# A graph-attention layer beside a dot-product layer: a list scheduler in the source orders the engines, and layer 1's value products go in halves among its scores

## The chip, the cores and the metric

The kernel runs on one core of one Trainium2 chip. The metric is the device time of one execution in microseconds. The core has a tensor engine (PE, with its weight loads shown as PEld), a vector engine (DVE), a scalar engine (ACT), GpSimd (POOL) and a sync engine (SP) that issues most DMAs. Each engine takes its instructions in the order in which the program wrote them.

## The reference

Eight entries (B = 8) of 2048 nodes with 256 channels pass through two layers, all in float32. `adj` is one 2048 x 2048 matrix of 0 and 1.

```python
# layer 0: eight heads of 32 channels, additive scores
x_proj = einsum('bnd,hdf->bhnf', x, W)
e = leaky_relu(e_src[..., :, None] + e_dst[..., None, :], 0.2)
e = e + softplus(beta_tilde) * log(adj + 1e-6)
attn = softmax(where(adj > 0, e, -big), axis=-1)
h = einsum('bhij,bhjf->bhif', attn, x_proj)        # heads side by side
x = layernorm(x + h @ W_out.T)
# layer 1: one head of 256 channels, dot-product scores
h1, h2, h3 = x @ W1, x @ W2, x @ W3
e = where(adj > 0, leaky_relu(h1 @ h2.T, 0.2), -1e12)
x = layernorm(x + relu(softmax(e, axis=-1) @ h3))
```

## The kernel before

**Layer 0** is cut into units. A unit is one entry, a pair of heads (`hp`, four of them) and one half of the 2048 rows (`rh`), so an entry has 8 units. A unit has 16 steps (`jt`), one for each block of 128 source nodes. A step has a tile `s` of 128 x 2 x 1024: for 11 of the 16 steps ACT first scales a mask tile `mt` that SP has loaded (L491, once per head), DVE then forms the attention weights from `c`, `re` and the scaled tile (L505, once per head), and POOL adds them into `sums` (L511, once per head). The other five steps are "direct": they skip ACT and POOL. PE takes each step with `products` (L537): four matmuls of 32 columns for the values (`val`) and, for a direct step, four more for the denominators (`den`). These are the **strips**. At a unit's end four more strips with `ones` close the sums (`close`). Seven `s` tiles are in use at most, four `mt` tiles, and `c` lies in two PSUM tiles that ACT fills once per unit (L501).

**Layer 1** goes row tile by row tile, 16 in an entry. A row tile has four score tiles (`e`, L715, full-width matmuls of 512 columns), each taken out of PSUM by ACT with the leaky ReLU (L717). DVE masks the row and finds its maximum (L724), ACT takes the exponential (L727). PE then transposes the result in four groups (`pt`, L743), ACT copies each out (`pts`, L745), and 16 products with `h3` add up in one PSUM tile (`acc`, L765). The row ends with a ReLU, a sum and a layernorm on ACT and DVE (L766 to L790).

Between the entries lies the **seam**: the output projection `y` of layer 0 (L411), its sum and layernorm (L415 to L439, and a store `x_d` issued from ACT's queue at L441), the transposes `tr` (L458) and `h3p` (L464), and the first query tiles (`h1p`, L704).

Layer 0 of entry 0 runs alone. From then on layer 1 of entry b-1 and layer 0 of entry b share the engines, in an order that is written out by hand: `Dot.step` writes for each quarter of a row tile a transpose of this row tile, a score tile of the next, and then `stream.feed()`, which takes one layer-0 step and makes another.

```python
self.scores(it + 1, lambda c: (turned(c), stream.scale_head() if c else None),
            lambda c: (stream.feed(), stream.scale_next(2) if c == NB - 1 else None))
...
for n in (7, 7, 7, 7, 6, 8, 7, 7, 7, 7, 8, 6, 7, 7):
    dot.step(stream, n)
```

The 16 products of `acc` follow in one piece after the fourth score tile. Full-width results rotate through two PSUM banks; the other six hold `val`, `den` and the two `c` tiles. Layer 1 of entry 7 has no layer 0 beside it, and there the two banks become six.

Of the kernel before, what the change touches and what calls it, by code (L numbers as in the profile page):

```python
# [18 lines left out]
P = 128  # L19
# [8 lines left out]
def kernel(  # L28
# [41 lines left out]
    LEAD = 3  # L70
    AHEAD = 1
# [8 lines left out]
    ps = ctx.enter_context(tc.tile_pool(name="ps", bufs=2, space=PSUM))  # L80
    pacc = ctx.enter_context(tc.tile_pool(name="pacc", bufs=1, space=PSUM))

    banks = ["mm"]

    def mm_tile(name):
        tag = banks[0]
        banks.append(banks.pop(0))
        if tag == "mm":
            return ps.tile([P, BK], F32, tag="mm", name=name)
        return pacc.tile([P, BK], F32, tag=tag, name=name)  # L90
# [139 lines left out]

    def mask(it, make):

        pen = wide_tile("pen", "pen", 1, BF16)
        if not make:
            nc.sync.dma_start(pen, pen_d[ts(it, P), :])
            return pen, lambda: None
        edges = [chunk.tile([P, HALF], I32, tag="ht", name="adj_r", bufs=4) for _ in range(2)]
        for s, a in enumerate(edges):
            nc.sync.dma_start(a, adj[ts(it, P), ts(s, HALF)])

        def put():
            nc.scalar.activation(pen[:, ts(0, HALF)], edges[0], AF.Relu, bias=no_edge, scale=-NO_EDGE)
            nc.vector.tensor_scalar(pen[:, ts(1, HALF)], edges[1], 0.0, NO_EDGE, ALU.is_le, ALU.mult)
            nc.sync.dma_start(pen_d[ts(it, P), :], pen)
        return pen, put
# [17 lines left out]
    class Gat:  # L263
# [132 lines left out]
        def load_rows(self, g):  # L396

            if g < NB:
                xg = chunk.tile([P, IG, D], F32, tag="ht", name="xg", bufs=4)
                nc.sync.dma_start(xg, x[self.b].rearrange("(t p) d -> p t d", p=P)[:, ts(g, IG), :])  # L400
                self.xs = getattr(self, "xs", []) + [xg]

        def rows(self, g):


            self.load_rows(g + 2)
            self.st = st = small.tile([P, IG // 2, nc.vector.BN_STATS_DIM], F32, name="st4", bufs=2)
            ys = [mm_tile("y").rearrange("p (t c) -> p t c", t=2) for _ in range(IG // 2)]
            for k in range(IG):
                for kc in range(KC):  # L410
                    nc.tensor.matmul(ys[k // 2][:, k % 2, :], self.ht[kc][:, ts(g * IG + k, P)], wot[:, kc, :],  # L411
                                     start=(kc == 0), stop=(kc == KC - 1))
            for k, y in enumerate(ys):
                z = self.x1(2 * g + k)
                nc.vector.tensor_add(z, y, self.xs[g][:, ts(k, 2), :])  # L415
            self.rows_factor()
            for k in range(len(ys)):
                nc.vector.bn_stats(st[:, k, :], self.x1(2 * g + k).rearrange("p t c -> p c t"))

        def rows_scale(self):  # L420

            self.mv = mv = self.st.rearrange("p a (t c) -> p (a t) c", t=2)
            self.f = f = small.tile([P, 2, IG], F32, name="f4", bufs=2)
            nc.scalar.activation(f[:, 0, :], mv[:, :, 2], AF.Ln, bias=eps_ln, scale=1.0 / D)
            nc.scalar.activation(f[:, 0, :], f[:, 0, :], AF.Exp, scale=-0.5)

        def rows_factor(self):

            if self.mv is not None:
                nc.vector.scalar_tensor_tensor(self.f[:, 1, :], self.mv[:, :, 1], -1.0, self.f[:, 0, :], ALU.mult, ALU.mult)  # L430
                self.mv = None

        def rows_end(self, g):

            self.rows_factor()
            for k in range(IG):
                z, f = self.x1(2 * g + k // 2), self.f
                row = z[:, k % 2, :]
                nc.scalar.activation(row, row, AF.Identity, bias=f[:, 1, k:k + 1], scale=f[:, 0, k:k + 1])  # L439
                if k % 2:  # L440
                    nc.scalar.dma_start(x1_d[self.b].rearrange("(t p) d -> p t d", p=P)[:, ts(2 * g + k // 2, 2), :], z)  # L441

# [3 lines left out]

        def turn(self):


            self.x1t = x1t = whole.tile([P, KC, N], F32, tag="x1t", name="x1t")  # L450
            self.h3 = h3 = whole.tile([P, NT, D], F32, tag="h3", name="h3")
            lag = 2 if self.b + 1 < B else 4
            for j in range(NT // 2 + lag):
                if j < NT // 2:
                    t = mm_tile("tr1")
                    for kc in range(KC):
                        for i in range(2):
                            nc.tensor.transpose(t[:, ts(kc * 2 + i, P)], self.x1(j)[:, i, ts(kc, P)], ident)  # L458
                    nc.scalar.copy(x1t[:, :, ts(j, 2 * P)], t.rearrange("p (k i) -> p k i", k=KC))
                if j >= lag:  # L460
                    t = mm_tile("h3p")
                    for i in range(2):
                        for kc in range(KC):
                            nc.tensor.matmul(t[:, ts(i, D)], x1t[:, kc, ts(2 * (j - lag) + i, P)], w3s[:, kc, :],  # L464
                                             start=(kc == 0), stop=(kc == KC - 1))
                    nc.scalar.copy(h3[:, ts(j - lag, 2), :], t.rearrange("p (i c) -> p i c", i=2))
                if j > 0:
                    yield

# [132 lines left out]
    class Stream:  # L602


        def __init__(self):
            self.units = [Unit(gats[b], hp, rh) for b in range(1, B) for hp in range(NP) for rh in range(2)]
            self.count = len(self.units) * NT
            self.loaded = self.scaled = self.made = self.eaten = 0
            self.held, self.heads = False, 0
            self.mts = {}  # L610

        def at(self, n):
            return self.units[n // NT], n % NT

        def load(self, upto):

            while self.loaded < min(upto, self.count):
                n = self.loaded
                self.mts[n] = load_mt(n // 2 % NT, n % 2)
                self.loaded += 1  # L620

        def scale_head(self, ahead=AHEAD):

            if self.heads == 0 and self.scaled < min(self.made + 1 + ahead, self.count, self.eaten + SLOTS):
                assert self.scaled - self.eaten < SLOTS
                unit, jt = self.at(self.scaled)
                unit.begin(jt, self.mts.pop(self.scaled))
                unit.scale(jt, 0)
                self.heads = 1

        def scale_next(self, ahead=AHEAD):

            self.scale_head(ahead)
            if self.heads:
                unit, jt = self.at(self.scaled)
                for a in range(1, HP):
                    unit.scale(jt, a)
                self.heads = 0
                self.scaled += 1

        def make_next(self):

            unit, jt = self.at(self.made)
            unit.make(jt)
            if jt == 4:
                stage_after(unit)
            self.made += 1
            self.load(self.made + 4)

        def ahead(self, count=1):  # L650

            for _ in range(count):
                self.scale_next()
                if self.made == self.scaled:
                    continue
                if self.made % NT == 0 and self.made and not self.held:
                    self.held = True
                    continue
                self.make_next()
                if self.held:  # L660
                    self.held = False
                    self.scale_next()
                    self.make_next()

        def eat(self, count=1):

            for _ in range(min(count, self.count - self.eaten)):
                unit, jt = self.at(self.eaten)
                assert self.eaten < self.made
                unit.eat(jt)  # L670
                evict()
                if jt == 0 and self.eaten > 0:
                    self.at(self.eaten - 1)[0].close()
                self.eaten += 1
                if self.eaten == self.count:
                    unit.close()
                if self.eaten % 2 == 0:
                    tick()
                    k = unit.rh * J2 + jt // 2
                    unit.gat.next_values(unit.hp, k)  # L680
# [9 lines left out]
    class Dot:  # L690
# [17 lines left out]
        def scores(self, it, between=lambda c: None, after=lambda c: None):  # L708

            (pen, put), p = mask(it, self.b == 0), self.p  # L710
            for c in range(NB):
# [6 lines left out]
                if c == 2:  # L718
                    put()
# [241 lines left out]
```

## Time and profile before

| | us |
|---|---|
| median of 3 runs | 4308.99 (4303.66 to 4311.37) |
| the profiled execution, its own time | 4305.87 |
| its span, first to last instruction | 4304.1 |
| PE busy | 4111.9 (96%) |
| DVE busy | 3257.0 (76%) |
| ACT busy | 2932.1 (68%) |
| POOL busy | 2910.7 (68%) |

Busy time of PE is the union of its matmuls, whose ends are modelled: a matmul that starts a little late because the array was being changed over does not show as idle. The starts of matmuls in the timeline are the better measure. A group line gives busy time, the mean duration of one instruction in ns, and the idle time of the engine before it with what ended that.

### The profile page before, as it was taken

The page shows a single profiled execution, that of the slowest core. Times are in us where ns is not written, and L with a number is a line of the kernel's source. Part 1 is how long each engine was busy: PE and PEld are TensorE (multiplying, and loading weights), DVE is VectorE, ACT ScalarE, POOL GpSimd, SP SyncE. Part 2 cuts the span into 40 slices and gives each one's busy share as a digit, 9 for nine tenths or more (in the row PEclk, how much of TensorE's full clock was granted, in tenths as well). Part 3 has the DMA queues.
Part 4 walks back from the last instruction along what each step waited for, and adds up shares of the span by engine and source line. Part 5 has one row for each costly group of instructions (what it writes and reads, how often), then busy time and mean ns, then how long its engine had stood idle before and what let it go on. Part 6 is the DMA issues. An engine that isn't in the chain of part 4 may idle for free.

```text
span 4304.1 us, 60568 instructions
## 1 busy us (share of the span) xinstructions
PE 4111.9 (96%) x22704; PEld 2073.5 (48%) x22704; DVE 3257.0 (76%) x3391; ACT 2932.1 (68%) x4148; POOL 2910.7 (68%) x1190
## 2 busy tenths in 40 slices
PE   7999889999999999999899999999899999999999
PEld 4444334444444444445444454444444444444766
DVE  7888878888787878788777878788787877787222
ACT  6522377777777767777777767778677776776555
POOL 0000468988788877889788878888788888888000
PEclk9999999999999999999999999999999999999999
DMA  7888756776565556556556665656566665664211
GB/s 257 280 287 291 235 188 231 231 233 225 186 204 189 190 192 200 189 188 225 177 186 201 198 203 183 200 183 207 194 203 193 197 205 180 192 200 145 74 47 47
DMA packets 346439, 843.65 MB, mean 196 GB/s; under 512 B 49696, under 2 KB 166432, under 8 KB 346144
## 3 DMA queue, kind: packets, MB, share of 16 engines
q1 hardware_dynamic: 328736, 822.99, 58.9%
q10 hardware_dynamic: 17408, 16.78, 1.2%
q8 instruction: 178, 2.92, 0.3%
q14 instruction: 117, 0.96, 0.1%
HBM read 763.76 MB, written 75.37 MB: 195 GB/s over the span
## 4 chain that ended last, share of the span: by engine, by line
PE 71%; ACT 10%; DVE 7%; DMA 6%; issue 4%; SPq 1%; ACTq 1%; POOL 0%; DVEq 0%; POOLq 0%
PE acc L765 18%; PE e L715 18%; PE val L537 16%; PE den L537 6%; PE pt L743 5%; ACT s L491 4%; DVE s L505 4%; DMA mt<-mt_d 3%; PE h1p L704 3%; PE y L411 2%; DVE p L724 2%; PE proj L296 1%; ACT c L501 1%; ACT ht L439 1%; PE h3p L464 1%
## 5 line engine op out<-in xcount | busy, mean ns | idle before, releaser
L511 POOL TENSOR_TENSOR sums<-sums,s 128x1024 f32<-128x1024 f32 x1008 | 2520.4, 2537 | 165.3 <-DVE s L505 164.3
L505 DVE SCALAR_TENSOR_TENSOR s<-c,re,s 128x1024 f32<-128x1024 f32 x1232 | 1502.5, 1273 | 316.9 <-ACT c L501 251.4
L491 ACT ACTIVATE s<-mt,re 128x1024 f32<-128x1024 f32 x1232 | 1358.7, 1143 | 92.8 <-DMA mt<-mt_d 76.2
L537 PE MATMUL val<-s,v 128*32 128x512 f32 x8192 | 1116.0, 607 | 81.6 <-DVE s L505 74.9
L715 PE MATMUL e<-x1t,h 128*128 128x512 f32 x2048 | 973.2, 598 | 20.7 <-ACT p L717 11.4
L765 PE MATMUL acc<-h,pts 128*128 128x256 f32 x4096 | 916.4, 382 | 4.4 <-ACT pts L745 4.3
L765 PEld LDWEIGHTS acc<-h,pts 128*128 128x128 f32 x4096 | 769.0, 190 | 200.6 <-ACT p L717 38.6
L505 DVE SCALAR_TENSOR_TENSOR s<-c,re,mt 128x1024 f32<-128x1024 f32 x560 | 688.3, 1271 | 0.2
L724 DVE CUSTOM_DVE_ANT_0 p<-p,pen 128x2048 f32<-128x2048 f32 x128 | 415.8, 3248 | 357.0 <-ACT p L717 356.9
L511 POOL TENSOR_TENSOR sums<-s 128x1024 f32<-128x1024 f32 x112 | 292.6, 2634 | 426.4 <-DVE s L505 419.2
L537 PEld LDWEIGHTS val<-s,v 128*32 128x32 f32 x8192 | 203.0, 109 | 746.4 <-issue 430.2
L715 PEld LDWEIGHTS e<-x1t,h 128*128 128x128 f32 x2048 | 348.4, 190 | 300.7 <-issue 248.0
L717 ACT ACTIVATE p<-e 128x512 f32<-128x512 f32 x512 | 305.4, 597 | 268.4 <-PE e L715 260.3
L537 PE MATMUL den<-s,re 128*32 128x512 f32 x3264 | 440.7, 593 | 0.0
L743 PEld LDWEIGHTS pt<-ident,p 128*128 128x128 f32 x2048 | 220.2, 141 | 424.1 <-ACT p L717 148.4
L745 ACT COPY pts<-pt 128x512 f32<-128x512 f32 x512 | 295.1, 580 | 145.0 <-PE pt L743 144.2
L727 ACT ACTIVATE p<-p,neg 128x2048 f32<-128x2048 f32 x128 | 256.1, 2001 | 199.3 <-DVE neg L725 148.4
L743 PE MATMUL pt<-ident,p 128*128 128x128 f32 x2048 | 328.6, 284 | 36.8 <-ACT pts L745 28.0
L505 DVE SCALAR_TENSOR_TENSOR s<-c_in,re,mt 128x1024 f32<-128x1024 f32 x256 | 310.1, 1277 | 48.5 <-DMA mt<-mt_d 35.9
L307 POOL PARTITION_ALL_REDUCE top<-top x8 | 6.6, 819 | 431.2 <-DVE top L306 414.6
L537 PEld LDWEIGHTS den<-s,re 128*32 128x32 f32 x3264 | 109.6, 110 | 244.5 <-issue 242.5
L298 ACT COPY v<-proj 128x512 f32<-128x512 f32 x64 | 37.2, 585 | 186.1 <-PE proj L296 135.9
(99 smaller groups left out, 2502.2 us busy)
## 6 DMA issues: line engine op xcount, KB each, us to landing
mt<-mt_d SPq DMA_DIRECT2D x992, 512.0 KB
c_in<-c_d SPq DMA_DIRECT2D x64, 1024.0 KB
pen<-pen_d SPq DMA_DIRECT2D x112, 512.0 KB
xg<-in_x_dram SPq DMA_DIRECT2D x60, 512.0 KB
adj_t<-in_adj_dram SPq DMA_DIRECT2D x16, 1024.0 KB
mt_d<-mt SPq DMA_DIRECT2D x32, 512.0 KB
rb<-rec_d SPq DMA_DIRECT2D x128, 128.0 KB
x_d<-ht ACTq DMA_DIRECT2D x64, 256.0 KB
```

The lines of the kernel that those rows point to most:

```text
L491: nc.scalar.activation(self.s[jt][:, a], self.mt[jt], AF.Copy, scale=self.gat.re[:, 1, jt, h:h + 1])
L505: nc.vector.scalar_tensor_tensor(s[:, a], self.c[a], self.gat.re[:, 0, jt, h:h + 1], m, ALU.max, ALU.mult)
L511: nc.gpsimd.tensor_tensor(self.sums[:, a], of[:, a], s[:, a], ALU.add)
L537: nc.tensor.matmul(dst[ts(q, DH), :], weights[q % 2], s[:, q % 2, ts(q // 2, BK)], start=start, stop=stop)
L704: nc.tensor.matmul(t, w12[:, kc, ts(dc, P)], self.x1t[:, kc, ts(g, BK)], start=(kc == 0), stop=(kc == KC - 1))
L715: nc.tensor.matmul(t, self.h1[:, kc, ts(it % IG, P)], self.x1t[:, kc, ts(c, BK)], start=(kc == 0), stop=(kc == KC - 1))
L717: nc.scalar.activation(p[:, ts(c, BK)], t, AF.Prelu, alpha=ALPHA)
L724: nc.vector.tensor_tensor_reduce(p, p, pen, 1.0, -FMAX, ALU.subtract, ALU.max, neg)
L727: nc.scalar.activation(p, p, AF.Exp, bias=neg, accum_out=den)
L743: nc.tensor.transpose(t[:, ts(k, P)], p[:, ts(g * IG + k, P)], ident)
L745: nc.scalar.copy(pt, t)
L765: nc.tensor.matmul(acc, pts[g][:, ts(k, P)], self.h3[:, j, :], start=(j == 0), stop=(j == NT - 1))
```

## The change

Layer 0 of entry 0 and all the setup stay. From entry 1 on every instruction is written by a list scheduler in the source. Each piece of work is a `Task` with a queue, a duration, the tasks that it needs and the buffers that it takes and frees. `Sched.run` keeps a clock per engine, always starts the task that can begin first, and so writes out the order for all five engines. The set of instructions is the same on each engine, with one exception: the 64 stores `x_d` are issued by SP and no longer by ACT.

Three rules of the scheduler bear on PE. Full-width work is a queue in fixed order, from which only seam work may be taken out of order within eight places. Strips are a second queue. `choose_pe` goes from one kind to the other by how far the strips lag behind a goal, with different limits while it is in strips (`LOW`) and in full work (`HIGH`, or `STRICT` where the next full task is not `easy`).

In layer 1 the 16 products of a row tile are cut into eight pieces of two, and from the second quarter on they stand one before and one after each score tile. The PSUM tile of `acc` is taken at the first piece and given back after the row's sum.

```diff
-    banks = ["mm"]
+    banks = ["m0", "m1"]
...
-        def feed(self, count=1):
-
-            for _ in range(count):
-                self.eat()
-                self.ahead()
...
+    LATE = 0.15
+    TURN = 0.13
+    WINDOW = 8
+    LOW, HIGH, STRICT = -1.0, 1.5, 4.0
+    QUEUES = {"ACT": (("copy", 0.0), ("relu", 0.3), ("evict", 0.3), ("ends", 0.4), ("exp", 0.9), ("c", 0.4), ("scale", 0.45), ("norm", 0.25)),
...
+            lag = self.goal(self.work) - self.eaten
+            if v[0] <= now + 0.1:
+                easy = self.full[0].easy
+                if f[0] > now + 0.35 or lag > (LOW if self.kind == "strip" else HIGH if easy else STRICT):
+                    return v[0], v[1], 0
+                return f[0], "full", f[1]
...
+    bank = Slots(2, ["m0", "m1"])
+    ring, mts, pts_s, hts, rows_s = (Slots(n, None, name) for n, name in ((SLOTS, "ring"), (4, "mt"), (4, "pts"), (4, "ht"), (4, "rows")))
...
-                if k % 2:
-                    nc.scalar.dma_start(x1_d[self.b].rearrange("(t p) d -> p t d", p=P)[:, ts(2 * g + k // 2, 2), :], z)
+                def store(k=k, g=g):
+                    nc.sync.dma_start(x1_d[b].rearrange("(t p) d -> p t d", p=P)[:, ts(2 * g + k, 2), :], gat.x1(2 * g + k))
...
-            acc = mm_tile("acc")[:, 0:D]
-            for g in range(NB):
-                for k in range(IG):
-                    j = g * IG + k
-                    nc.tensor.matmul(acc, pts[g][:, ts(k, P)], self.h3[:, j, :], start=(j == 0), stop=(j == NT - 1))
...
+            if h == 0:
+                hold = r["ah"] = Hold(bank, 1)
+            t = pe("full", "acc", 0.89, mm, deps, hold, easy=(h > 6))
...
+            for c in range(NB):
+                turn(it, c)
+                if c and b + 1 < B:
+                    acc(it, 2 * c - 2)
+                if more:
+                    scores(it + 1, c)
+                if c and b + 1 < B:
+                    acc(it, 2 * c - 1)
+            if more:
+                soft(it + 1)
+            for h in range(6 if b + 1 < B else 0, 8):
+                acc(it, h)
...
+    span = 303.0
+    S.goal = lambda w: NP * 2 * NT * (w + 33.0) / span
+    S.run()
```

In the new code `T` is the transpose group that was `pt`, and `h1`, `h3`, `tr`, `y` and `e` are as before.

## The prediction

> **What bounds the kernel now.** I read the page first.
>
> ```profile
> span 4304.1 us, 60568 instructions
> PE 4111.9 (96%) x22704; PEld 2073.5 (48%) x22704; DVE 3257.0 (76%) x3391; ACT 2932.1 (68%) x4148; POOL 2910.7 (68%) x1190
> PE 71%; ACT 10%; DVE 7%; DMA 6%; issue 4%; SPq 1%; ACTq 1%; POOL 0%; DVEq 0%; POOLq 0%
> ```
>
> PE is busy nearly throughout and holds 71% of the chain of waits. Then the busy times by stage, for an entry in the middle (PE, PEld, DVE, ACT, POOL, clock, DMA):
>
> ```profile
> 1994.00:2491.00 497.00, 481.53 (x2630) 234.56 (x2632) 396.46 (x414) 368.16 (x507) 415.72 (x169) 0.99 0.60 196
> ```
>
> The next engine, POOL, has 81 us to spare in 497. But busy time hides how well PE runs, so I read the starts of its groups, in the streamed part and in entry 7, which has no strips:
>
> ```profile
> 2222.75 1.06 PE L537 MATMUL val<-s,v 128*32 128x512 f32 x8
> 2223.74 0.66 PE L743 MATMUL pt<-ident,p 128*128 128x128 f32 x4
> 2224.24 1.88 PE L715 MATMUL e<-x1t,h 128*128 128x512 f32 x4
> 2226.05 1.06 PE L537 MATMUL val<-s,v 128*32 128x512 f32 x8
> ...
> 4100.42 0.60 PE L743 MATMUL pt<-ident,p 128*128 128x128 f32 x4
> 4100.86 1.88 PE L715 MATMUL e<-x1t,h 128*128 128x512 f32 x4
> 4102.58 0.60 PE L743 MATMUL pt<-ident,p 128*128 128x128 f32 x4
> ```
>
> Unmixed, pt takes 0.44 us and e 1.72. Mixed with one strip product a round takes 3.30. A strip product is 0.86 inside a run of them (24 matmuls in 2.78 us), so 0.29 us of the round is no work: it is the price of going from full width to strips and back, 0.146 per change.
>
> An entry's work at unmixed prices: 176 strip products x 0.87 = 153, 64 e 110, 64 pt 28, 16 acc x 6.9 = 110, y and h3p 28, h1p 14, tr 3: 446 us. The order of the built program has 186 changes in an entry: 27 us. That leaves 24 us of waits. The largest stands in every seam:
>
> ```profile
> 2048.95 1.09 ACT L439 ACTIVATE ht<-ht,f 128x256 f32<-128x256 f32 x2 [0.44 <-ACT ht L439]
> ...
> 2051.91 1.99 ACT L501 COPY c<-c_in 128x1024 f32<-128x1024 f32 x2
> ...
> 2054.33 2.27 PE L537 MATMUL val<-s,v 128*32 128x512 f32 x5 [6.67 <-DVE s L505]
> ```
>
> The strips wait for DVE, DVE for the new unit's `c`, and ACT copies that only after the seam's normalisations and their stores. Around it (2041 to 2060) the granted clock is 0.82, in the whole entry 0.99: some 3.4 us more. So 10 of the 24 us are the seam, 14 are spread.
>
> **The change, part by part**, against the profiled execution's own 4306 us (3 below the median).
>
> *Fewer changes.* The order of the changed program has the same matmuls and 791 stretches of one kind instead of 1375: 584 x 0.146 = -85 us, all on PE's path. Around y the first interval is longer (0.17 per change), so -80 to -98.
>
> *The seam.* In the changed order ACT has scales and `c` copies between the normalisations, and the 64 stores `x_d` are off its queue. I take away 7 x 10.4 = -73. Put back: y tiles come in pairs in two banks, each pair waits for two DVE sums (0.69 each), and strip blocks of three to six products can outrun DVE (1.21 us per head, four in 4.85). Bounds: nothing, or the old 10.4 per entry; I take 6, nearer the old row since DVE's sums are no faster: +42. The stores cost SP 64 x 0.37 = 24 us; behind one that waits for its normalisation stand mt loads, covered by the four mt tiles; without that cover it is in the lateness term below.
>
> *One bank instead of two.* acc keeps a bank from its first piece to the row's sum, so T and e take turns in the other, and each must be read out before the next may start. Only two products of acc (0.86) lie between. The price of a handover:
>
> ```profile
> 2220.44 0.66 PE L743 MATMUL pt<-ident,p 128*128 128x128 f32 x4
> ...
> 2220.93 1.88 PE L715 MATMUL e<-x1t,h 128*128 128x512 f32 x4
> ...
> 2221.14 0.59 ACT L745 COPY pts<-pt 128x512 f32<-128x512 f32 x1 [1.61 <-PE pt L743]
> ...
> 2222.85 0.60 ACT L717 ACTIVATE p<-e 128x512 f32<-128x512 f32 x1 [1.13 <-PE e L715]
> 2223.35 2.18 ACT L491 ACTIVATE s<-mt,re 128x1024 f32<-128x1024 f32 x2
> ```
>
> ACT starts 1.92 us after e's start and reads for 0.60; with 0.05 to release PE the bank is free at 2.57, and e plus two acc products last 2.58. After pt (0.06 less without a change) it is free at 1.28 against 1.30. So it just fits, if ACT is free at that moment. I counted what the changed order puts on ACT between the two reads at the 440 handovers that have nothing but acc as cover. Scales follow each other at 1.04, a read holds ACT for 0.50. Nothing between: no wait. Two scales between T and e: ready at 3.21 against 3.22, no wait. One scale between e and T: 0.24 late, 70 times, 17 us. A row's ending (0.28 + 0.20 + 0.29 + 0.60 = 1.38): after two scales 1.38 late, 18 times, 25 us; after or before one 0.34, 22 times, 7 us; between e and T 0.58, 14 times, 8 us. `c` between e and T, 8 times: 1 us. And 67 times acc's first piece stands right behind e and T and needs e's bank: 2.57 against 2.16, 0.41 late, 28 us. Sum +86.
>
> *The old spread waits* (14 x 7 = -98) belong to an order that is gone; if half have causes that stay, it is -49.
>
> *The end of a row tile.* From the last e to the next T lie one ACT read, the mask, the exponential:
>
> ```profile
> L724 DVE CUSTOM_DVE_ANT_0 p<-p,pen 128x2048 f32<-128x2048 f32 x128 | 415.8, 3248 | 357.0 <-ACT p L717 356.9
> L727 ACT ACTIVATE p<-p,neg 128x2048 f32<-128x2048 f32 x128 | 256.1, 2001 | 199.3 <-DVE neg L725 148.4
> ```
>
> 0.63 to the read, 0.60, 3.25, 0.15, 2.00, 0.19 and five releases: 7.1, and with a scale or a make in the way about 7.8 (estimate: half of each). Before, all of acc (6.9) and strips covered it. Now three pieces of acc (2.6) and a strip block do. Of 110 boundaries the order covers 14 by 6.7, 21 by 7.6, 21 by 7.9 to 8.7, the others by over 9. As the mask takes 2.3 to 4.2 us, the short ones wait about 1 us and the next about 0.5: +35 (15 to 60).
>
> *Lateness from elsewhere.* ACT's queue is in order: a scale that waits for its mt tile now delays the reads behind it, and PE. Before, ACT waited 76 us in all for mt. Bounds 0 and 76; I take 3 per entry, nearer none since four tiles stay ahead: +21.
>
> *The end.* Strips run out one row tile before layer 1 of entry 7 in both orders. Then two boundaries stand nearly bare: 3.0 and 0.4 us of cover for 6 to 7, where before a whole acc and the last h3p lay. +9.
>
> Entry 0's layer 0 is unchanged: 0, give or take 10 for the handover.
>
> Sum: -85 - 73 + 42 + 86 - 98 + 35 + 21 + 9 = -63, so 4243 profiled and **4246** as a median. An entry becomes about 487 us; POOL needs 415 of it and DVE 396, so neither becomes the bound.
>
> A rule against this change: the Trainium skill, "TensorE: Matmul & The Clock Gate", section "A second HAM failure mode: psum-queue depth-cycling", says that a PE which idles a little between groups as it cycles through PSUM banks can fall back to half its clock again and again. Here the clock was 1.00 in the streamed stretch from 600 to 1022 us and fell only around waits as long as the seam's; the new waits are at most 1.4 us. By the rule, one 6.8 us stretch at half clock per row tile would be 112 x 3.4 = 380 us and the time about 4630, as an estimate. I go by the row.
>
> **The rivals.**
>
> *ACT arrives late at the bank (slower).* The counts above suppose that ACT reaches each read with only its written work in the way. If its scales slip, each of the 440 handovers meets one in progress. Scales fill 41% of ACT's time (1359 of some 3340 us), the mean rest is 0.52: 0.21 per handover at random, +94; at every one 0.52, +229 instead of 59. So 4340 to 4416, taken as 4355. It decides from 0.14 us more per handover (63 / 440). For it: the margins are 0.01 to 0.02 us. Against: ACT is 74% busy in an entry and idles before most reads.
>
> *The waits go away (much faster).* No seam wait and no exposed row end, as strips fill every gap: -85 - 73 - 98 + 86 + 9 = -161, 4148. For it: all other engines have 80 us to spare per entry. Against: cover at the row ends is short by count.
>
> *It comes out even.* Blocks of strips wait for DVE as the seam does now: 9 us per entry cancel the gain, 4300 to 4317. For it: seven `s` tiles against blocks of five steps. Against: DVE has 100 us to spare per entry.
>
> That the change does not do what it says is excluded by the order: 584 changes fewer, pieces of two among the scores.
>
> **How the numbers follow.** This measurement tells 0.2% (9 us) from no change. Forecast 0.50 (4200 to 4295, all but 0.04 of it faster), much faster 0.12, even 0.06 (0.04 of it within 0.2%), ACT late 0.32. Faster 0.58, same 0.08, slower 0.34. The range takes in most of the late-ACT case and goes down to where the waits nearly vanish: 4160 to 4365.
>
> **What would show it.** Right: the wait of val for s at the seam gone; entries of about 487 us; PE waiting for ACT's p and pts some 12 us per entry where the old waits were 52 in all; T waiting for the exponential a few times per entry. Wrong: handover waits of 0.5 us all over (ACT late); half clock in row tiles; val waiting for s in the blocks (DVE).

## The result, and the profile after

The changed kernel takes 4328.5 us (median of 9 runs, 4315.1 to 4338.0), the kernel before 4304.4 in runs on the same chip. The ratio is 1.0049 (95% interval 1.0032 to 1.0065): slightly slower, where 4246 and faster was forecast. The profiled run of the changed kernel is the quickest of its nine, 4315.1, so its trace shows somewhat less than what the median lost.

The head of the page after, and the shares of the chain of waits by engine:

```profile
span 4313.3 us, 60790 instructions
PE 4076.4 (95%) x22704; PEld 2114.0 (49%) x22704; DVE 3297.6 (76%) x3391; ACT 2930.5 (68%) x4148; POOL 2854.5 (66%) x1190
PE 54%; ACT 14%; DVE 9%; DMA 7%; issue 4%; POOL 1%; SPq 0%; ACTq 0%; DVEq 0%; POOLq 0%
```

PE has lost 35 us of busy time (4111.9 before), as fewer changes should have it, yet the span has grown by 9. Its share of the chain of waits fell from 71% to 54%: more of the run is now spent with another engine ending last. The waits view of PE says which waits these are. First the longest line of before, then the first four of after (total us, times, longest):

```profile
PE val L537 <- DVE s L505: 74.9, 26, 10.5
```

```profile
PE T L1165 <- ACT p L1142: 67.2, 30, 11.4
PE acc L1184 <- ACT p L1097: 26.5, 69, 3.1
PE T L1165 <- ACT p L1097: 21.5, 18, 3.0
PE e L1091 <- ACT pts L1170: 17.9, 17, 4.1
```

The seam's wait for `s` is gone, as forecast. Of the four lines of after, the last three are handovers of the single bank, forecast too. The first of the four is the end of the row: T waits for the exponential, 30 times, up to 11.4 us. The prediction had that wait at 0.5 to 1 us a time. The longest of them, in the timeline of after (start, length, engine, line, what; in brackets the idle time before):

```profile
1940.36 18.60 POOL L888 TENSOR_TENSOR sums<-sums,s 128x1024 f32<-128x1024 f32 x8
...
1944.07 1.96 PE L1091 MATMUL e<-x1t,h 128*128 128x512 f32 x4
...
1946.69 14.41 DVE L1136 CUSTOM_DVE_ANT_0 p<-p,pen 128x2048 f32<-128x2048 f32 x1
...
1961.40 2.00 ACT L1142 ACTIVATE p<-p,neg 128x2048 f32<-128x2048 f32 x1 [11.17 <-DVE neg L1137]
...
1963.55 1.11 PE L1165 MATMUL T<-ident,p 128*128 128x128 f32 x4 [11.36 <-ACT p L1142]
...
1964.46 3.62 PE L1091 MATMUL e<-x1t,h 128*128 128x512 f32 x4
```

The mask (L1136) takes 14.41 us. The same instruction takes 2.29 when POOL is idle. All that time POOL runs adds back to back: eight between 1940.4 and 1959.0, of which five began after the mask had. Here the mask ran only when POOL had no more adds. `e` at the end takes 3.62 against 1.96 at the top: PE came out of its wait at half clock. The stretch by the granted clock (us, then busy time of PE, PEld, DVE, ACT, POOL, clock):

```profile
1954.70:1968.40 13.70, 4.85 (x11) 2.68 (x12) 12.60 (x12) 4.87 (x6) 6.62 (x3) 0.50 0.32 105
```

So a late mask costs three times: the exponential and T are late by it; the makes queued behind it on DVE are late, so there are soon no strips to fill the gap; and afterwards PE runs a while at half clock.

The Trainium skill, "SBUF — State Buffer", section "Who interferes with whom", says that a DVE instruction with two SBUF inputs and a GpSimd instruction that reads SBUF exclude each other, and that whichever issues first holds the pair for its whole length. The trace agrees in part: an add whose turn comes while a mask runs is recorded as 4.4 us in place of 2.38 (91 adds before, 65 after). But a waiting mask did not always get the pair when the running add ended: adds that began later went ahead of it, up to five in a row.

How often does this happen? Of the masks that begin while an add runs, 2 of 110 let a further add pass in the profile before (longest mask 6.47), 14 of 93 after (12 of them over 5 us, the longest 14.41). One difference between the two orders can be counted in the traces: the adds whose `s` is already made when such a mask begins. Before there are 1.0 on the mean and never over 3, as make and add go in step; after 1.9 and up to 7, as the planner lets the makes run ahead of POOL. The planner knew that the two exclude each other (the mask's task has `lock=True`, which keeps POOL's clock back), but that lives in the plan alone: on the chip nothing made the adds wait. In the 14.41 case all five adds stand behind the mask in the planner's order. In the profile before, both adds that passed a mask stand ahead of it in the program.

To see what that is worth, I added up PE's time in each profiled run from the starts of its groups: each interval less the shape's own (`e` 0.429 a matmul, strips 0.107) goes to a change of shape, to half clock, or to a wait by what ended it. "Row end" is T waiting for the exponential, "bank" a wait until ACT has read a PSUM bank out, "seam" the other waits between entries, "strips for DVE" a strip waiting for `s`. "Restart" is a long interval with no releaser named, mostly the first of an `e` (0.53 in place of 0.43 us after a wait, and after some 60% of the acc pieces too); "start" is the stretch up to 600 us. Work is 3800 us in every kernel, and 18 to 29 us of small leftovers are in no column.

| us | changes (times) | row end | bank | seam | strips for DVE | restart | start | half clock |
|---|---|---|---|---|---|---|---|---|
| before | 207 (1374) | 0 | 61 | 25 | 49 | 25 | 96 | 19 |
| after | 128 (790) | 72 | 101 | 30 | 3 | 30 | 86 | 34 |
| e1_turn | 128 (790) | 24 | 88 | 32 | 0 | 29 | 86 | 23 |
| e4_acc_end | 164 (992) | 22 | 77 | 40 | 3 | 21 | 87 | 31 |
| e6_turn_acc_end | 163 (992) | 13 | 72 | 29 | 2 | 21 | 85 | 21 |
| e7_turn_alt | 272 (1692) | 50 | 46 | 16 | 11 | 20 | 88 | 22 |
| e8_turn_long | 97 (618) | 23 | 87 | 37 | 3 | 32 | 90 | 22 |
| e9_turn_end_long | 122 (754) | 18 | 86 | 27 | 8 | 23 | 94 | 17 |
| e10_turn_late_long | 109 (688) | 17 | 80 | 23 | 0 | 24 | 87 | 15 |
| e11_long_only | 97 (618) | 86 | 93 | 34 | 4 | 33 | 92 | 45 |

### The profile page after: what moved, and what is told of

It reads as the page before. It is cut to its first block, busy times and chain, and to the rows that moved or that the text cites. A ratio compares the mean times of both kernels' runs of the same rounds, so it can differ in the third digit from the quotient of the medians.

```text
span 4313.3 us, 60790 instructions
## 1 busy us (share of the span) xinstructions
PE 4076.4 (95%) x22704; PEld 2114.0 (49%) x22704; DVE 3297.6 (76%) x3391; ACT 2930.5 (68%) x4148; POOL 2854.5 (66%) x1190
## 4 chain that ended last, share of the span: by engine, by line
PE 54%; ACT 14%; DVE 9%; DMA 7%; issue 4%; POOL 1%; SPq 0%; ACTq 0%; DVEq 0%; POOLq 0%
PE e L1091 17%; PE acc L1184 15%; PE val L445 10%; ACT s L399 6%; DMA mt<-mt_d 6%; DVE p L1136 5%; PE T L1165 4%; PE den L445 4%; DVE s L880 3%; PE h L1041 2%; PE h L1067 2%; ACT p L1097 2%; ACT p L1142 2%; ACT pts L1170 1%; POOL sums L888 1%
## 5 line engine op out<-in xcount | busy, mean ns | idle before, releaser
L888 POOL TENSOR_TENSOR sums<-sums,s 128x1024 f32<-128x1024 f32 x1008 | 2488.5, 2507 | 248.2 <-DVE s L880 207.6
L445 PE MATMUL val<-s,v 128*32 128x512 f32 x8192 | 1036.2, 601 | 36.4 <-DVE s L880 12.2
L1184 PE MATMUL acc<-h,pts 128*128 128x256 f32 x4096 | 1031.9, 385 | 27.0 <-ACT p L1097 26.5
L1091 PE MATMUL e<-x1t,h 128*128 128x512 f32 x2048 | 1000.1, 613 | 20.7 <-ACT pts L1170 17.9
L1136 DVE CUSTOM_DVE_ANT_0 p<-p,pen 128x2048 f32<-128x2048 f32 x128 | 460.4, 3597 | 533.0 <-ACT p L1097 532.8
L445 PEld LDWEIGHTS val<-s,v 128*32 128x32 f32 x8192 | 232.7, 109 | 568.3 <-issue 446.2
L888 POOL TENSOR_TENSOR sums<-s 128x1024 f32<-128x1024 f32 x112 | 270.4, 2436 | 263.2 <-DVE s L880 254.0
L1165 PE MATMUL T<-ident,p 128*128 128x128 f32 x2048 | 325.3, 283 | 92.7 <-ACT p L1142 67.2
L1165 PEld LDWEIGHTS T<-ident,p 128*128 128x128 f32 x2048 | 238.4, 142 | 306.9 <-ACT p L1142 98.0
L1170 ACT COPY pts<-T 128x512 f32<-128x512 f32 x512 | 296.7, 580 | 89.3 <-PE T L1165 88.6
```

Source lines behind the costliest of these rows:

```text
L445: nc.tensor.matmul(dst[ts(q, DH), :], weights[q % 2], s[:, q % 2, ts(q // 2, BK)], start=start, stop=stop)
L888: nc.gpsimd.tensor_tensor(u.sums[:, a], of[:, a], u.s[jt][:, a], ALU.add)
L1091: nc.tensor.matmul(t, box["h"][:, kc, ts(it % IG, P)], gat.x1t[:, kc, ts(c, BK)], start=(kc == 0), stop=(kc == KC - 1))
L1136: nc.vector.tensor_tensor_reduce(p, p, r["pen"], 1.0, -FMAX, ALU.subtract, ALU.max, neg)
L1165: nc.tensor.transpose(t[:, ts(k, P)], pbox["p"][:, ts(c * IG + k, P)], ident)
L1170: nc.scalar.copy(pt, t)
```

## The experiments

Theory A: the gain was there and the late masks ate it. Theory B: the single bank's handovers ate it (101 us is after's largest wait). All ratios are to the kernel before, with their 95% interval.

**e1_turn: give the mask its turn.** The planner remembers the last mask's `neg`, and the next add is preceded by a small GpSimd copy that reads it. So POOL cannot begin an add that the plan has behind the mask.

```
-                r["neg"] = neg = small.tile([P, 1], F32, name="neg")
+                r["neg"] = S.guard = neg = small.tile([P, 1], F32, name="neg")
...
+                        if S.guard is not None:
+                            nc.gpsimd.tensor_copy(small.tile([P, 1], F32, name="turn", bufs=1), S.guard)
+                            S.guard = None
                         nc.gpsimd.tensor_tensor(u.sums[:, a], of[:, a], u.s[jt][:, a], ALU.add)
```

> The changed kernel, with one small GpSimd copy of neg after each mask, which makes the adds that the plan put behind a mask wait for it. Theory A (the mask loses its turn to queued adds, and the row end that is late by it eats the gain): no mask is passed by an add that the plan has behind it, none is over about 7 us (15 of 128 were above 5 us, the longest 14.41), TensorE's waits for the exponential in mid-run fall from 63 us to about 20 and its slow clock from 25 us to about 10, and the time falls by 45 to 64 us, from 4328 to 4265 to 4285, which is faster than before (4304). Theory B (one bank for e, T and the eviction's lateness eat it): the waits in the spread, about 92 us, are what they were; the time moves by less than 15 us and stays at 4313 to 4330. Third possibility: the adds now wait for a late mask and the closing products come late, slower than 4328.

Measured: 4242.5 us, ratio 0.9849 (0.9826 to 0.9873), 86 less than the changed kernel and more than theory A had asked for. The mask's group in after, and in e1 with the copy (busy us, mean ns; idle time before and its releaser):

```profile
L1136 DVE CUSTOM_DVE_ANT_0 p<-p,pen 128x2048 f32<-128x2048 f32 x128 | 460.4, 3597 | 533.0 <-ACT p L1097 532.8
```

```profile
L1140 DVE CUSTOM_DVE_ANT_0 p<-p,pen 128x2048 f32<-128x2048 f32 x128 | 367.2, 2869 | 533.7 <-ACT p L1101 533.5
L890 POOL COPY turn<-neg 128x1 f32<-128x1 f32 x110 | 20.3, 184 | 279.1 <-DVE neg L1141 279.1
```

The masks are 93 us shorter in sum, one of 128 is over 5 us (5.69). POOL pays 20 us for the copies and 279 in waiting, and it can afford that: it is busy 65% of the span, and the only wait put down to the copies is 1.5 us of PE's weight loads. PE's waits for the exponential:

```profile
PE T L1169 <- ACT p L1146: 22.1, 17, 5.4
```

67.2 us became 22.1. In the table the row end fell by 48, half clock by 11; the bank's waits, 101 to 88, fell too, probably because ACT comes late to its reads where the row end is late. Together these are 72 of the 76 us between the two profiled runs. Theory B said that the time would move by less than 15 us: it does not explain the loss.

**e2_max_after and e3_max_before: the same by other means, and a control.** The pass over two inputs is replaced by a plain maximum over one; the subtraction of the penalty is left out, so an instruction that does not meet POOL stands in the mask's place.

```
-                nc.vector.tensor_tensor_reduce(p, p, r["pen"], 1.0, -FMAX, ALU.subtract, ALU.max, neg)
+                nc.vector.tensor_reduce(neg, p, mybir.AxisListType.X, ALU.max)
```

> The changed kernel with the mask's pass over two inputs put by a plain row maximum of p: the subtraction of the penalty is left out, all instructions of the other engines stay. Theory A: every mask is 2.1 to 2.4 us long (3.85 on the mean before, up to 14.41), no add is held up either; the row end is 1.5 us shorter on the mean and never long: 4240 to 4270. Theory B: only the mean matters, 1.5 us at each of some 45 rows where TensorE now waits for the exponential, at most 63 us in all and about half of it: 4295 to 4315, and the bank's waits stay at about 92 us.

> The kernel before with the same edit (plain row maximum, the subtraction of the penalty left out), as the control. Both theories: the masks of before are hardly ever passed (2 of 97) and TensorE has cover at its row end, so the time stays within 10 us of 4304. If it falls by as much as the changed kernel's with this edit does, the mask is not what makes the two kernels differ.

Measured: e2 4236.8 us, 0.9837 (0.9816 to 0.9859); e3 4280.5 us, 0.9933 (0.9918 to 0.9948). The group of e2:

```profile
L1136 DVE TENSOR_REDUCE neg<-p 128x1 f32<-128x2048 f32 x128 | 292.5, 2285 | 535.6 <-ACT p L1097 535.4
```

Every pass now takes 2.29 us. e2 lands 3 us under theory A's range (4240 to 4270), far from theory B's (4295 to 4315) and 6 us from e1: once the mask keeps its turn, its remaining 0.6 us of waiting is worth little. The control missed its expectation: before gained 25 us where at most 10 were allowed. Its seam waits fell from 25 to 12 and its bank waits by 5, so the kernel before also pays something for masks that wait for one add. But the changed kernel gains 92 from the same edit. With this edit in both kernels, the planner's order is worth 44 us (4280.5 to 4236.8), less than the 62 that the forecast gave it.

**e5_before_turn: the copy in the kernel before.** If the copy were of use in itself, it would show here.

```
             neg = small.tile([P, 1], F32, name="neg")
+            asked.append(neg)
...
+                    if asked:
+                        nc.gpsimd.tensor_copy(small.tile([P, 1], F32, name="turn", bufs=1), asked.pop())
+                        asked.clear()
                     nc.gpsimd.tensor_tensor(self.sums[:, a], of[:, a], s[:, a], ALU.add)
```

> The kernel before with the same small GpSimd copy of neg after each mask as in e1. Theory A (the changed kernel's masks lose their turn, those of before hardly: 2 of 110, none above 6.5 us): nothing to win, 4296 to 4310. If the copy is of use in itself (GpSimd held back, SBUF traffic thinned) it falls here by as much as in e1, 60 to 90 us: 4215 to 4245.

Measured: 4312.2 us, 1.0013 (1.0004 to 1.0021): no gain, 2 us outside the expected range on the slow side. Seven masks of 110 were passed here (longest 8.31), by work of POOL that stands ahead of them in the program, which a copy behind the mask cannot hold back. A long mask should also hurt it less, as after the last score it has all of acc, 6.9 us, to do; e4 tests that for the changed kernel.

**e4_acc_end: acc whole at the row's end.** The eight pieces of acc stand after the last score, as in the last entry. That frees the second bank for T and e, and covers the row's end.

```
                 turn(it, c)
-                if c and b + 1 < B:
-                    acc(it, 2 * c - 2)
                 if more:
                     scores(it + 1, c)
-                if c and b + 1 < B:
-                    acc(it, 2 * c - 1)
...
-            for h in range(6 if b + 1 < B else 0, 8):
+            for h in range(8):
```

> The changed kernel with layer 1's value products (acc) not in halves among the scores but all eight pieces after the row's last score, as the last entry has them; the planner decides the rest. Two banks are then free for T and e. Theory B: the handovers of the single bank (T to acc, acc to T, acc to e, about 92 us) fall to below 40, nothing else is lost, and the time is 4235 to 4260. Theory A: the long masks stay (10 to 20 of 128 above 5 us) but are covered by 6.7 us of products in place of 1.7, so that the waits for the exponential fall from 63 us to below 25; the waits of T and e for their evictions come back in another place (before had about 98 us of them in the spread): 4270 to 4310.

Measured: 4264.1 us, 0.9896 (0.9879 to 0.9914), just under A's range and over B's. Nine of 101 masks are passed here too, up to 11.36 us, but the row end costs 22 us in place of 72: work that covers the row end takes most of the cost of long masks away, though not the half clock (31 us). The bank's waits fell only from 101 to 77. They have moved:

```profile
PE e L1091 <- ACT p L1097: 48.2, 125, 5.0
```

With acc away, nothing but T lies between one score and the next.

**e6_turn_acc_end: both.**

> e1 and e4 together: adds wait for the mask, and acc's eight pieces stand after the row's last score, so that T and e have two banks. 990 changes of shape in place of 788: +202 x 0.146 = +29 us. Theory B (one bank is dear): the handovers of e1 (33 T to acc, 27 acc to T, 22 acc to e, 83 us) go, e4's T to e (61 us) stays: 4240 or less. Theory A with the bank's price as the prediction had it, taken back by as much waiting in T to e: e4's waits for the exponential are only 17 us, so the turn wins at most 10 to 20 us on e4's 4264: 4245 to 4262, slower than e1.

Measured: 4229.9 us, 0.9820 (0.9807 to 0.9834). A's price was 15 us too high. B's time (4240 or less) came, but not in the way that B gave: against e1 the bank's waits are only 16 less, but the row end is 11 less, the restarts 8, and small leftovers not in the table 10; that pays for 35 us of changes. The copy is worth 34 us to e4 and 86 to the changed kernel: what late masks cost depends on how much work covers the row end.

**e7_turn_alt and e8_turn_long: the price of a change.** e1 with the planner's thresholds moved, so that it goes between strips and full width more, or less, often.

```
-    LOW, HIGH, STRICT = -1.0, 1.5, 4.0
+    LOW, HIGH, STRICT = 0.5, 0.5, 0.5        (e7)
+    LOW, HIGH, STRICT = -3.0, 3.0, 5.0       (e8)
```

> e1 with the planner's three thresholds all at 0.5, so that strips and row tiles alternate as soon as the strip is behind: 1690 changes of shape in the program in place of 788. At 0.146 us a change, 902 x 0.146 = +132 us, 4374; finer strips may cover evictions that stand bare in e1 (83 us of handovers), so 4330 to 4375. If a change costs nothing where it falls beside a wait, less than +60: below 4300.

> e1 with the thresholds at -3, 3 and 5 (longer blocks): 616 changes in place of 788, 172 x 0.146 = -25 us. If the blocks still stand where the row ends need them 4217 to 4230; if the longer blocks leave row ends or handovers without cover, up to +20 back: 4230 to 4260.

Measured: e7 4339.8 us, 1.0077 (1.0064 to 1.0090); e8 4221.3 us, 0.9801 (0.9788 to 0.9814); both as expected. e7 has 902 changes more than e1 and 144 us more for them, 0.160 each, near the prediction's 0.146; 28 us of waits went (42 at the bank, while the row end rose by 26). e8 has 172 fewer and gained 21, of the 25 priced.

**e9_turn_end_long, e10_turn_late_long, e11_long_only: what goes together.** e9 is e6 with e8's thresholds. e10 is e8 with acc begun two scores later:

```
-                if c and b + 1 < B:
-                    acc(it, 2 * c - 2)
+                if c > 1 and b + 1 < B:
+                    acc(it, 2 * c - 4)
...
-                if c and b + 1 < B:
-                    acc(it, 2 * c - 1)
+                if c > 1 and b + 1 < B:
+                    acc(it, 2 * c - 3)
...
-            for h in range(6 if b + 1 < B else 0, 8):
+            for h in range(4 if b + 1 < B else 0, 8):
```

e11 is the changed kernel with e8's thresholds and no copy.

> e6 with e8's thresholds (-3, 3, 5): the turn guaranteed, acc after the row's last score, longer blocks. 752 changes of shape in place of e6's 990: 238 x 0.146 = -35 us on e6's 4230. If longer blocks cost nothing else 4190 to 4200; if they take cover from T to e (60 us bare in e6 already) or from the seams, up to 20 back: 4200 to 4220, about e8's 4221 or a little under.

> e8 with acc's pieces begun two scores later (the last four after the row's last score): 686 changes in place of e8's 616, +10 us; the bank is held by acc for about half as long as in e8, so of the handovers there (35 + 22 + 19 = 76 us) some 30 go and half of e6's T to e (30) comes: no gain, 4220 to 4235. If one bank is dear beyond that (e6 beat e1 by 12 us in spite of 29 us of changes), 4195 to 4215.

> The changed kernel with e8's thresholds and without the copy of neg. Theory A: the masks lose their turn as in the changed kernel (10 to 20 of 128 above 5 us) and about 80 us are lost again against e8's 4221: 4290 to 4315. If the blocks and not the turn had made e8, 4225 to 4250.

Measured: e9 4220.1 us, 0.9804 (0.9791 to 0.9816), the upper end of what was expected: of 41 us of changes saved, the bank took 14 back, and start and strips 15. e10 4185.9 us, 0.9723 (0.9706 to 0.9740), under both expectations and the best of all: against e8, changes cost 12 more, but seam 14, restart 8, bank and half clock 7 each, row end 6 and start 3 less. Its waits:

```profile
PE e L1095 <- ACT p L1101: 23.2, 73, 1.5
PE T L1169 <- ACT p L1146: 16.3, 8, 5.8
PE T L1169 <- ACT p L1101: 13.0, 11, 2.4
```

That half the acc gives up T to acc and takes T to e was as expected (an even exchange at the bank); why seam and restarts also fell was not tested.

e11 4278.6 us, 0.9932 (0.9908 to 0.9957), 11 below A's range and 29 above the rival's. Its runs spread from 4256.8 to 4314.3, those of e8 from 4217 to 4226. The profiled run is the longest:

```profile
PE T L1165 <- ACT p L1142: 89.3, 26, 10.8
```

14 masks of 96 are passed, up to 15.62 us, and row end and half clock take 131 us where e8 has 45. So the kernel without the turn loses 57 us on the median and 94 in this run: as I read it, whether a mask is passed varies from run to run, which also makes the time uneven; only one run of each kernel has a trace, so that is not shown.

## Why the prediction was wrong

The sum came out: e1, which is the change with the masks in the planner's order, takes 4242, and the forecast was 4246. Much of that is luck. By the table, seam, bank and old spread waits (with strips, restart and half clock) came to -7 in e1 where -73 + 42 + 86 - 98 = -43 stood; row end, lateness and end came to +24 where 35 + 21 + 9 = +65 stood. The two errors nearly cancel. By its steps:

*Fewer changes*, -85: 79 by the table, right.

*The end of a row tile*, +35 (15 to 60), is **the step that failed**. It took the mask at "2.3 to 4.2 us", from the group's mean and one add to wait for, though the profile before already had masks of 6.12 and 6.47. With the turn kept the term is 24, the last entry's waits included; in the changed kernel it is 72, with half clock 11 us and bank 13 above e1's. A bound was taken from the group's mean. What sets the worst case is not the mask's own row but POOL's queue: it was five adds long here, and 5 x 2.33 with the rest of the running add (0.72) and the mask's 2.29 makes 14.7, against 14.41 measured. I counted in the changed order what lies on ACT between two reads of the bank, but not what lies on POOL when a mask falls due.

*The old spread waits*, -98, failed too. They were taken to vanish with the old order. Bank, seam and restart made 111 us of them; the bank's 61 have their successor in the term below, but seam and restart (25 and 25 us) did not vanish: they are 30 and 30 in after. The first `e` after a wait, 0.1 us longer, had no term at all.

*The seam*, -73 and +42: the wait for `s` went from 49 to 3, and the seam's others rose by 5 only. So 42 was put back where 5 was due, which hid most of the last error.

*Lateness from elsewhere*, +21, is not told apart by the table. ACT's waits for `mt` were 76 us in all before, 92 in after and 87 in e1; what they cost PE was not measured.

*One bank instead of two*, +86: 88 in e1, right, and in the lines named. The time moved the way of the rival "ACT arrives late at the bank" (slower, 4340 to 4416), but its cause did not come: its 94 us more are not in after's 101. The rival "It comes out even" (4300 to 4317) was as near in time, but its wait, strips for DVE, is 3 us.

*The clock*: half clock came in after in 18 stretches of 3.4 to 13.7 us from 600 us on, 34 us lost in all against 19 in before. All but the last stand beside a wait of PE of 1.8 to 11.4 us, nine of them for the exponential; shorter bank waits have none. The 380 us that one stretch per row tile would have cost did not come. I had gone by the row and taken the new waits as short (1.4 us at most): that step fell with the row end's.

*An entry*, 487 us: 499 in after, 489 in e1, 497 before. The signs named for "right" were all there (no `s` wait at the seam, bank waits, 14 us an entry for the 12 named). Of the signs for "wrong" one came, half clock in row tiles; that it would come from a late mask was not thought of.

## What to carry to other kernels

A plan that keeps two engines apart in its own clocks keeps nothing apart on the chip: where two instructions exclude each other and one of them ends a chain that the bound engine waits for, give the other a real dependency. Here one copy of 0.18 us per row was worth 2%; in the kernel before, where the adds that pass a mask stand ahead of it in the program, it was worth nothing. When you price an instruction that shares a resource, do not take the mean of its group; take the shortest, the longest, and the queue that can stand before it in the new order. Before a fine-grained rearrangement is given up for a small loss, look for one wait that has eaten it: with the turn and two settings moved, the same planner is 2.8% faster than before.

## What the runs showed of the hardware

A DVE instruction that waits for one of POOL's adds is not always served next: adds of 2.38 us that began after it, up to five in a row, went first. In most cases (64 of 93 in after) the mask got in at the next add's end although another was ready. What decides it is open: where in the running add the mask began (0 to 2.3 us) shows no pattern, and the number of ready adds does not by itself decide it: with two adds ready, none of 25 masks was passed in before and 7 of 22 in after. Nor is it tested why before loses fewer (2 of 110, and 7 of 110 in e5) than the planner's orders without the copy (14 of 93 in after, 9 of 101 in e4, 14 of 96 in e11).
